# Rows of turns in DRAM once instead of twice, and stacked queries by two transfers instead of four

## The chip, the cores and the metric

The kernel runs on one core of one Trainium2 chip. The time is device microseconds (us) of a whole execution. The kernel before took 3939.81 us, the median of three runs between 3923.31 and 3940.42. Profiles come from one execution; a "line" (L951) is a line of the kernel's source.

## The reference

A single layer of a vision transformer runs on 16 images of 512 x 512, each cut into N = 1024 patches of 768 values and embedded to E = 256. The part that this change touches is attention with 8 heads of 32, whose keys go through a Fourier series before they meet the queries:

```
q, k, v = split(layernorm(h) @ w_qkv)            # 8 heads of 32
k = sum over f = 1..256 of kan_a[f]*sin(f*k) + kan_b[f]*cos(f*k)
h = h + softmax(q @ k.T / sqrt(32)) @ v @ w_out + b_out
h = h + shared_mlp(layernorm(h)) + two best of four experts(layernorm(h))
```

Everything is float32. Per image there are 256 x 1024 key values, each with 256 sines and 256 cosines.

## The kernel before

**The series.** The 256 frequencies are split into products of slow and fast waves. A key value is turned into a whole number of 2^-32 turns (the *turns*, `ui`), and a second one a quarter turn ahead (`uh`); the product of such an integer with a frequency wraps by itself. Eight key rows (`e`) make a group `g`; an image has 32 groups (`NG`) and the kernel 512. A group has two tiles `w` of 128 lanes x 1024 (j = 0, 1) of slow waves, four rows each, and one tile `f` of fast waves. Each goes through POOL (turn times the lane's frequency, L1006), ACT (sine, L1016), and then PE mixes the two w tiles (`mix`, L1036), DVE multiplies by f (L1050), and PE adds up (`add_up`, L1069). Four groups make a *round*; there are 128, and one step of attention (`att`: a pair of heads and half of the queries) runs two rounds behind its keys: eight score steps (L1134), eight exponentials (L1149), eight weighings of the values (L1167).

**Through DRAM.** A lane of a w tile needs one of four rows, with or without the quarter turn, so rows have to be spread over lanes. This goes through DRAM:

- `keys` (L564 to L607) computes turns of 128 rows x 512 columns and writes `uh` and `ui` to `ud[E, 2, 2, N]`: row, quarter or not (`f`), copy (`i`), column. Both copies come from one transfer that reads its source twice.
- `load_waves` (L942 to L956) fills a w tile by two loads, one for each half of the columns. The source is four rows x 2 x 2 copies = 16 rows of DRAM, each read by 8 lanes: a pattern of [16, 8, 512] with stride 0 in the middle; the destination is 128 partitions. There are 2048 such loads of 256 KB. A load waits until both halves of its rows are written and, with eight w tiles, until the mix of four groups before has freed its tile.
- `load_source` (L958 to L984) loads `src`, from which DVE spreads the fast waves' rows. It reads copy 0 in 512 loads of 64 KB, whose source pattern leads with the eight groups.
- `queries` (L619 to L641) writes queries, split into a high and a low part, to `qd[2, E, N]`. `stack_queries` (L1106 to L1122) fills `q4[128, 2, 512]` for one step of attention: for the high and the low part (j), each twice (x), 32 partitions. A score step multiplies it with stacked keys `k4`.
- `finish_keys` and `stack_keys` (L1082 to L1102) do the like for keys, by way of `kd`.

**What sets the order.** The order of PE's work is written out in a string (`ORDER`), one letter or digit for each step. The order on SP, POOL, ACT and DVE is made at build time by a planner (`others`, L408): it gives each step a cost and a time at which its dependencies are done, and takes the step that can start soonest. All of these transfers are issued by SP, in the planner's order; SP waits at each until what it depends on is done. `sent` and `transfer` (L312 to L320) are the planner's costs of transfers, and the numbers given to `put` those of issuing. They set the place of a step in its queue, and nothing on the chip.

Of the kernel before, what the change touches and what calls it, by code (L numbers as in the profile page):

```python
# [11 lines left out]
FP = mybir.dt.float32  # L12
# [6 lines left out]
P = 128  # L19
E = 256  # L20
NPAIR = 4
HD = 32
N = 1024
# [17 lines left out]
INT = mybir.dt.int32  # L41
# [10 lines left out]
PE, ACT, DVE, POOL, SP = "pe", "act", "dve", "pool", "sp"  # L52
# [38 lines left out]
def plain_path(ctx: ExitStack, tc: tile.TileContext, a: dict, out: bass.AP, verdict: bass.AP):  # L91
# [9 lines left out]
    nc = tc.nc  # L101
    xT = a["xT"]
    B = xT.shape[0]
    NG = N // P * 4

    def pool(name, bufs, space=None):
        kw = {} if space is None else {"space": space}
        return ctx.enter_context(tc.tile_pool(name=name, bufs=bufs, **kw))
# [4 lines left out]
    udp = pool("udp", 2, DRAM)  # L113
    qdp = pool("qdp", 2, DRAM)
# [17 lines left out]
    def load(shape, src, name):  # L132
        t = const.tile(shape, FP, tag=name, name=name)
        nc.scalar.dma_start(out=t, in_=src)
        return t
# [4 lines left out]
    def halves(src):  # L140
        return src.rearrange("(c p) e -> p c e", p=P)
# [4 lines left out]
    w_qkv = a["w_qkv"]  # L146

    wk = load([P, 2, E], halves(w_qkv[:, E : 2 * E]), "wk")
    wq = load([P, 2, E], halves(a["wq"]), "wq")
# [20 lines left out]
    for i in range(4):  # L170
        nc.scalar.dma_start(out=biases[ds((NE + 1) * i, NE), 0, :], in_=a["eb3"])
        nc.scalar.dma_start(
            out=biases[ds((NE + 1) * i + NE, 1), 0, :], in_=a["sb3"].unsqueeze(0)
# [78 lines left out]
    done = {}  # L252
# [8 lines left out]
    def put(engine, queue, cost, deps, key, action):  # L261

        queues[engine].setdefault(queue, []).append((cost, deps, key, action))
# [29 lines left out]
    def side_tile(name):  # L293

        i = chains[now["chain"]]["bank"] = banks(now["chain"])[0][1]
        return side.tile([P, 512], FP, tag=f"side{i}", name=name)
# [15 lines left out]
    def transfer(took, issue=0.0, ready=0.0):  # L312

        clock[SP] = max(clock[SP], ready) + issue
        now["dma"] = max(now["dma"], clock[SP]) + took
        return now["dma"] + LANDS

    def sent(took, issue):

        return transfer(took, issue, chains[now["chain"]]["ready"])  # L320
# [154 lines left out]
    images = [{} for _ in range(B)]  # L475
# [88 lines left out]
    def keys(b, rows, blks=(0, 1)):  # L564

        st = images[b]
        if b >= 2:
            yield "load", NG * (b - 1) - 1, 1
            yield "source", (NG * (b - 1)) // 8 - 1
        if "ud" not in st:  # L570
            st["ud"] = udp.tile([E, 2, 2, N], INT, tag="ud", name="ud")
        for blk in blks:
            yield "hnT", b, blk
            yield ANY
            ps = side_tile("k")
            for c in range(2):
                matmul(
                    out=ps,
                    lhsT=wk[:, c, ts(rows, P)],
                    rhs=hnT[:, c, ts(blk, 512)],  # L580
                    start=(c == 0),
                    stop=(c == 1),
                )
            held = chains[now["chain"]]["bank"]
            yield DVE, 1.4
            chains[now["chain"]]["bank"] = held
            u = rup.tile([P, 512], FP, tag="u", name="u")
            n = u.bitcast(INT)
            nc.vector.tensor_scalar(n, ps, INV_2PI, None, ALU.mult)
            nc.vector.scalar_tensor_tensor(ps, n, -TWO_PI_A, ps, ALU.mult, ALU.add)  # L590
            yield DVE, 1.4
            chains[now["chain"]]["bank"] = held
            for part in (TWO_PI_B, TWO_PI_C):
                nc.vector.scalar_tensor_tensor(ps, n, -part, ps, ALU.mult, ALU.add)
            yield DVE, 1.4
            ui = rup.tile([P, 512], INT, tag="r", name="ui")
            uh = n
            nc.vector.tensor_scalar(u, ps, INV_2PI_REST * 2.0**31, None, ALU.mult)
            nc.vector.scalar_tensor_tensor(ui, ps, INV_2PI * 2.0**31, u, ALU.mult, ALU.add)
            yield POOL, 1.02  # L600
            nc.gpsimd.tensor_tensor(uh, ui, quarter.to_broadcast([P, 512]), ALU.add)
            for i, x in enumerate((uh, ui)):
                nc.sync.dma_start(
                    out=st["ud"][ts(rows, P), i, :, ts(blk, 512)],
                    in_=x.unsqueeze(1).to_broadcast([P, 2, 512]),
                )
            done["rows", b, rows, blk] = sent(2.7, 1.2)  # L607

    def split(src, name):

# [8 lines left out]
    def queries(b, rows):  # L619
        st = images[b]  # L620
        for half in range(2):
            yield "hnT", b, half
        if b >= 2:
            yield "q", 2 * NPAIR * (b - 1) - 1
        if rows == 0:
            st["qd"] = qdp.tile([2, E, N], FP, tag="qd", name="qd")
        for blk in range(2):
            yield ANY
            ps = side_tile("q")
            for c in range(2):  # L630
                matmul(
                    out=ps,
                    lhsT=wq[:, c, ts(rows, P)],
                    rhs=hnT[:, c, ts(blk, 512)],
                    start=(c == 0),
                    stop=(c == 1),
                )
            yield DVE, 1.4
            for i, x in enumerate(split(ps, "q")):
                nc.sync.dma_start(out=st["qd"][i, ts(rows, P), ts(blk, 512)], in_=x)  # L640
            done["queries", b, rows] = sent(1.4, 1.0)  # L641

    def values(b):
# [294 lines left out]
    def rows_of(g):  # L938
        b, g = divmod(g, NG)
        return [("rows", b, g // (NG // 2), blk) for blk in range(2)]  # L940

    def load_waves(g, j):  # L942


        def action():
            w = w_tiles[g, j] = wp.tile([P, N], INT, tag="w", name="w")
            ud = images[g // NG]["ud"]
            src = ud[ds(8 * (g % NG) + 4 * j, 4)].rearrange("e f i n -> (e f i) n")
            for c in range(2):
                part = src[:, ts(c, 512)].unsqueeze(1).to_broadcast([16, 8, 512])  # L950
                nc.sync.dma_start(out=w[:, ts(c, 512)], in_=part)  # L951
            done["loaded", g, j] = transfer(1.9)

        old = g - NW // 2
        deps = rows_of(g) + ([("mix", old)] if old >= 0 else [])
        put(SP, "waves", 1.1, deps, ("load", g, j), action)  # L956

    def load_source(p):  # L958


        def part(j, blk):
            def action():
                if j == blk == 0:
                    sources[p] = srcp.tile([P, 2, 512], INT, tag="src", name="src")
                ud = images[p // NPAIR]["ud"]
                rows = ud[ts(p % NPAIR, 64), :, 0, :].rearrange(
                    "(g j r e) f n -> j r g e f n", j=2, r=2, e=2
                )
                for r in range(2):
                    nc.sync.dma_start(  # L970
                        out=sources[p][ds(64 * j + 32 * blk, 32), r, :],
                        in_=rows[j, r, :, :, :, ts(blk, 512)],
                    )
                landed = transfer(0.4)
                if j == blk == 1:
                    done["source", p] = clock[SP]
                    done["angles", p] = landed

            return action

        deps = rows_of(8 * p) + [("spread", 8 * p - 1) if p > 0 else ("load", 0, 1)]
        for j in range(2):
            for blk in range(2):
                put(SP, "source", 1.4, deps, ("part", p, j, blk), part(j, blk))  # L984
# [121 lines left out]
    def stack_queries(att):  # L1106
        p, qb = divmod(att, 2)
        b, i = divmod(p, NPAIR)

        def action():  # L1110
            q4 = bands_of_queries[att] = q4p.tile([P, 2, 512], FPR, tag="q4", name="q4")
            for j in range(2):
                src = images[b]["qd"][j, ts(i, 64), ts(qb, 512)]
                for x in range(2):
                    nc.sync.dma_start(
                        out=q4.bitcast(FP)[ds(64 * j + HD * x, HD), :, :],
                        in_=src.rearrange("(s d) n -> d s n", s=2),
                    )
            done["q4", att] = transfer(1.6)

        deps = [("queries", b, i // 2)] + ([("score", att - 2, NT - 1)] if att > 1 else [])
        put(SP, "queries", 2.0, deps, ("q", att), action)  # L1122


    scores = {}
# [110 lines left out]
    for j in range(XBUFS):  # L1236
        load_x(0, j)
    feed(1, first_norm(0, 0), keys(0, 0, [0]))
    feed(0, first_norm(0, 1), keys(0, 0, [1]))
    for b in range(B):  # L1240
# [29 lines left out]
    for rd in range(B * RI + 2):  # L1270
        groups = range(GS * rd, min(GS * rd + GS, total))
        att = rd - 2
# [706 lines left out]
def _places():  # L1979

    d = np.arange(HD)
    return d // 16 * 8 + d // 8 % 2 * 2 + d // 4 % 2 * 16 + d // 2 % 2 * 4 + d % 2
# [56 lines left out]
```

## Time and profile before

| What | Before |
|---|---|
| Median of three runs | 3939.81 us |
| The profiled execution: its own time, and its span from the first to the last instruction | 3924.07 us, 3922.5 us |
| Granted TensorE clock, mean | 0.994 |
| Data moved by transfers | 916.51 MB, 234 GB/s on average |
| HBM read, written | 758.64 MB, 150.99 MB |
| Issue of one w load on SP, of one q load, of one src load (median) | 544 ns, 419 ns, 652 ns |
| First and last issue of a w load, from the span's start | 57.2 us, 3791.8 us |
| PE: weighing of values, scores, mixes (busy) | 1269.7 us, 707.6 us, 540.1 us |
| POOL: turns of w and f (busy) | 2893.8 us |

PE is the tensor engine (PEld its weight loads), ACT the scalar, DVE the vector, POOL the GpSimd and SP the sync engine; SPq is SP's queue, where transfers are issued. `w<-ud` is a transfer into tile w from ud. A row of waits names who waited, for whom, the time in all, how often, and the longest. The chain that ended last goes back from the last instruction to what released it, step by step, and gives the share of the span that each engine or line has in it. The share of a DMA queue is the time that its packets took, out of the time of 16 DMA engines.

### The profile page before, as it was taken

How to read it: one execution, taken by the hardware profiler on the slowest of the kernel's cores; microseconds unless marked ns; L12 is line 12 of the kernel's file. 1: busy time of each engine (PE TensorE's matmuls, PEld its weight loads, DVE VectorE, ACT ScalarE, POOL GpSimd, SP SyncE). 2: the span in 40 equal slices, each digit the busy share in tenths (PEclk: the TensorE clock that was granted, in tenths of full speed). 3: DMA queues.
4: the chain of work that ended last, by engine and by line, in shares of the span. 5: the costliest groups of instructions: out<-in, count | busy, mean ns of one | idle time of the engine just before them, and what ended most of it. 6: DMA issues, size and time to landing. Idle time of an engine off the chain costs nothing.

```text
span 3922.5 us, 102737 instructions
## 1 busy us (share of the span) xinstructions
PE 3810.0 (97%) x40337; PEld 1948.9 (50%) x40337; DVE 2531.7 (65%) x4075; ACT 3263.0 (83%) x3939; POOL 3193.6 (81%) x2328
## 2 busy tenths in 40 slices
PE   7899999999999999999999999999999999999998
PEld 4334454554545555455454545545455454544444
DVE  4656757667675766757667675776767767576652
ACT  2788888888888888888888888888888888888983
POOL 3998878788788878879788788878879888888860
PEclk9999999999999999999999999999999999999999
DMA  7987968888787888979889788798878889788860
GB/s 228 281 261 217 278 192 245 259 226 258 220 257 225 237 264 224 259 216 256 235 233 265 212 257 247 224 265 224 262 218 255 247 229 265 216 245 235 221 170 18
DMA packets 587615, 916.51 MB, mean 234 GB/s; under 512 B 58828, under 2 KB 177524, under 8 KB 587124
## 3 DMA queue, kind: packets, MB, share of 16 engines
q1 hardware_dynamic: 580880, 906.98, 80.6%
q8 instruction: 321, 5.26, 0.6%
q10 hardware_dynamic: 6244, 2.88, 0.3%
q14 instruction: 170, 1.39, 0.1%
HBM read 758.64 MB, written 150.99 MB: 232 GB/s over the span
## 4 chain that ended last, share of the span: by engine, by line
PE 66%; DMA 13%; ACT 8%; POOL 5%; DVE 4%; issue 3%; SPq 2%; ACTq 0%; POOLq 0%; DVEq 0%
PE av L1167 17%; PE sT L1134 10%; PE kan L1036 8%; DMA w<-ud 7%; PE red L1069 4%; PE e1p L301 3%; PE tok L301 3%; ACT w L1016 3%; POOL w L1006 3%; PE e3p L301 2%; PE tok L304 2%; DMA k<-kd 2%; PE s1p L301 2%; PE e1p L304 2%; ACT f L1016 2%
## 5 line engine op out<-in xcount | busy, mean ns | idle before, releaser
L1006 POOL TENSOR_TENSOR w<-w,lane 128x1024 int32<-128x1024 int32 x1024 | 1923.6, 1895 | 406.9 <-DMA w<-ud 275.7
L1149 ACT ACTIVATE es<-sT 128x1024 f32<-128x1024 f32 x1024 | 1014.3, 1022 | 357.3 <-PE sT L1134 312.2
L1016 ACT ACTIVATE w<-w 128x1024 f32<-128x1024 int32 x1024 | 1013.4, 1046 | 67.5 <-POOL w L1006 64.3
L1006 POOL TENSOR_TENSOR f<-f,lane 128x1024 int32<-128x1024 int32 x512 | 970.2, 1895 | 102.0 <-DVE f L991 84.8
L1134 PE MATMUL sT<-q,k 128*128 128x512 f32 x2048 | 707.6, 454 | 42.9 <-DMA k<-kd 13.4
L1050 DVE TENSOR_TENSOR f<-kan,f 128x1024 f32<-128x1024 f32 x512 | 605.2, 1214 | 203.1 <-ACT f L1016 116.3
L991 DVE STREAM_SHUFFLE f<-src 128x1024 int32<-128x1024 int32 x512 | 681.3, 1370 | 0.4
L1167 PE MATMUL av<-es,v 128*32 128x256 f32 x8192 | 638.8, 383 | 3.5 <-DVE rc L1208 2.6
L1167 PE MATMUL av<-es,ones 128*32 128x256 f32 x8192 | 630.9, 379 | 0.0
L1036 PE MATMUL kan<-w,coef 64*32 64x512 f32 x8192 | 540.1, 598 | 18.8 <-ACT w L1016 12.6
L1016 ACT ACTIVATE f<-f 128x1024 f32<-128x1024 int32 x512 | 519.0, 1046 | 4.1 <-POOL f L1006 4.1
L1134 PEld LDWEIGHTS sT<-q,k 128*128 128x128 f32 x2048 | 351.2, 190 | 340.0 <-issue 146.0
L1167 PEld LDWEIGHTS av<-es,v 128*32 128x32 f32 x8192 | 235.5, 109 | 343.2 <-issue 236.9
L1167 PEld LDWEIGHTS av<-es,ones 128*32 128x32 f32 x8192 | 267.2, 110 | 176.4 <-issue 1.4
L1191 DVE RECIPROCAL rc<-av 128x256 f32<-128x256 f32 x128 | 224.8, 1756 | 169.5 <-PE av L1167 169.5
L1036 PEld LDWEIGHTS kan<-w,coef 64*32 64x32 f32 x8192 | 129.1, 105 | 313.9 <-issue 133.4
L1069 PE MATMUL red<-f,pack 128*32 128x512 f32 x2048 | 271.0, 602 | 0.0
L301 PE MATMUL tok<-wt,x 128*128 128x256 f32 x768 | 182.1, 389 | 22.1 <-DMA w1s<-in_sW 12.5
L1016 ACT ACT_TABLE_LOAD x128 | 164.2, 1283 | 17.7 <-DMA w<-ud 15.5
L304 PE MATMUL tok<-wt,x 128*32 128x256 f32 x3072 | 178.0, 380 | 0.6 <-DVE h L548 0.6
L301 PEld LDWEIGHTS tok<-wt,x 128*128 128x128 f32 x768 | 147.4, 194 | 57.9 <-DMA w1s<-in_sW 12.4
L513 ACT ACTIVATE hn<-h,less,rstd 128x256 f32<-128x256 f32 x256 | 140.7, 591 | 39.8 <-POOL less L505 39.0
(148 smaller groups left out, 4269.5 us busy)
## 6 DMA issues: line engine op xcount, KB each, us to landing
w<-ud SPq DMA_DIRECT2D x2048, 256.0 KB
q<-qd SPq DMA_DIRECT2D x512, 128.0 KB
k<-kd SPq DMA_DIRECT2D x128, 512.0 KB
x<-in_xT SPq DMA_DIRECT2D x128, 384.0 KB
ud<-u SPq DMA_DIRECT2D x64, 512.0 KB
ud<-ui SPq DMA_DIRECT2D x64, 512.0 KB
src<-ud SPq DMA_DIRECT2D x512, 64.0 KB
qd<-qhi SPq DMA_DIRECT2D x64, 256.0 KB
```

What stands on the lines that cost most here:

```text
L301: nc.tensor.matmul(out=out, lhsT=lhsT, rhs=rhs, start=start, stop=stop)
L304: nc.tensor.matmul(out=out[ts(i, 32)], lhsT=lhsT[:, ts(i, 32)], rhs=rhs, start=start, stop=stop)
L991: nc.vector.stream_shuffle(w, sources[g // 8].rearrange("p r n -> p (r n)"), [4 * (g % 8) + i // 8 for i in range(32)],)
L1006: nc.gpsimd.tensor_tensor(w, w, f.to_broadcast([P, N]), ALU.mult)
L1016: nc.scalar.activation(x, w, AF.Sin, scale=TURN * 2.0**-32)
L1036: nc.tensor.matmul(out=ps[ds(64 * j + 32 * blk, 32), ts(r, 512)], lhsT=coef[ts(r, 64)].rearrange("p e f j -> p (e f j)"), rhs=w[ts(r, 64), ...
L1050: nc.vector.tensor_mul(w, kan.pop(g), w)
L1069: nc.tensor.matmul(out=rows_of_pair[p][ts(2 * i + r, 32), :], lhsT=pack[:, ds(PACK0 - 16 * (k % 2) - 2 * (k // 2), 32)], rhs=prod[:, ts(r, ...
L1134: nc.tensor.matmul(out=ps[:, ts(s, 512)], lhsT=k4[:, 2 * s + kc // 4, ts(kc % 4, P)], rhs=q4[:, s, :], start=True, stop=True,)
L1149: nc.scalar.activation(es, scores.pop(kc), AF.Exp, scale=SCALE)
L1167: nc.tensor.matmul(out=acc[0][ts(i, HD), ts(half, 256)], lhsT=ones32 if half else v[:, kc, p % NPAIR, ts(i % 2, HD)], rhs=es[:, ds(512 * ( ...
L1191: nc.vector.reciprocal(rc[0], acc[0][:, 256:512])
```

## The change

Turns' rows are written to DRAM once: `ud` loses its dimension of copies, and the write of a half of the rows goes from 512 KB to 256 KB. A w load has now 8 rows of DRAM, each read by 16 lanes: the source pattern goes from [16, 8, 512] to [8, 16, 512]. The bytes that a load puts into the tile stay the same, and so does the order of the lanes.

Queries lie in DRAM by halves of the columns and with the two heads of a pair interleaved (a row is d, then s), for which the columns of `wq` are put in another order before launch. A head pair's high or low part is then 32 runs of 1024 values, and one load fills 64 partitions by reading them twice: the source pattern leads with a dimension of size 2 and stride 0. A step of attention takes two loads of 256 KB instead of four of 128 KB.

The planner's costs of the rows' writes and of stacked queries are smaller; `ORDER` is the same.

```diff
-            st["ud"] = udp.tile([E, 2, 2, N], INT, tag="ud", name="ud")
+            st["ud"] = udp.tile([E, 2, N], INT, tag="ud", name="ud")
...
             for i, x in enumerate((uh, ui)):
-                nc.sync.dma_start(
-                    out=st["ud"][ts(rows, P), i, :, ts(blk, 512)],
-                    in_=x.unsqueeze(1).to_broadcast([P, 2, 512]),
-                )
-            done["rows", b, rows, blk] = sent(2.7, 1.2)
+                nc.sync.dma_start(out=st["ud"][ts(rows, P), i, ts(blk, 512)], in_=x)
+            done["rows", b, rows, blk] = sent(1.4, 1.0)
...
-            st["qd"] = qdp.tile([2, E, N], FP, tag="qd", name="qd")
+            st["qd"] = qdp.tile([2, 2, E, 512], FP, tag="qd", name="qd")
...
-                nc.sync.dma_start(out=st["qd"][i, ts(rows, P), ts(blk, 512)], in_=x)
+                nc.sync.dma_start(out=st["qd"][i, blk, ts(rows, P)], in_=x)
...
-            src = ud[ds(8 * (g % NG) + 4 * j, 4)].rearrange("e f i n -> (e f i) n")
+            src = ud[ds(8 * (g % NG) + 4 * j, 4)].rearrange("e f n -> (e f) n")
             for c in range(2):
-                part = src[:, ts(c, 512)].unsqueeze(1).to_broadcast([16, 8, 512])
+                part = src[:, ts(c, 512)].unsqueeze(1).to_broadcast([8, 16, 512])
                 nc.sync.dma_start(out=w[:, ts(c, 512)], in_=part)
...
-                rows = ud[ts(p % NPAIR, 64), :, 0, :].rearrange(
+                rows = ud[ts(p % NPAIR, 64)].rearrange(
                     "(g j r e) f n -> j r g e f n", j=2, r=2, e=2
                 )
...
-                src = images[b]["qd"][j, ts(i, 64), ts(qb, 512)]
-                for x in range(2):
-                    nc.sync.dma_start(
-                        out=q4.bitcast(FP)[ds(64 * j + HD * x, HD), :, :],
-                        in_=src.rearrange("(s d) n -> d s n", s=2),
-                    )
+                src = images[b]["qd"][j, qb, ts(i, 64)].rearrange("(d s) n -> d (s n)", s=2)
+                nc.sync.dma_start(
+                    out=q4.bitcast(FP)[ts(j, 64)].rearrange("p s n -> p (s n)"),
+                    in_=src.unsqueeze(0).to_broadcast([2, HD, 1024]),
+                )
...
-        put(SP, "queries", 2.0, deps, ("q", att), action)
+        put(SP, "queries", 1.1, deps, ("q", att), action)
...
-    heads = np.arange(0, E, HD)[:, None]
-    arrays["wq"] = arrays["w_qkv"][:, (heads + _places()).ravel()]
+    heads = np.arange(0, E, HD).reshape(NPAIR, 1, 2)
+    arrays["wq"] = arrays["w_qkv"][:, (heads + _places()[:, None]).ravel()]
```

## The prediction

> **What bounds the kernel now.** I read the page from the top: busy shares, slices, DMA queues, the chain that ended last. Then the list of DMA issues, the waits, and SP's queue in order of time in the middle of the run.
>
> Busy shares and DMA queues of the kernel before (share of the span; packets, MB, share of 16 DMA engines):
>
> ```profile
> PE 3810.0 (97%) x40337; PEld 1948.9 (50%) x40337; DVE 2531.7 (65%) x4075; ACT 3263.0 (83%) x3939; POOL 3193.6 (81%) x2328
> ...
> q1 hardware_dynamic: 580880, 906.98, 80.6%
> ...
> PE 66%; DMA 13%; ACT 8%; POOL 5%; DVE 4%; issue 3%; SPq 2%; ACTq 0%; POOLq 0%; DVEq 0%
> ```
>
> PE sets the pace (97%), at 3922.5/128 = 30.6 us for each of 128 rounds, but the 16 DMA engines are used to 80.6% *if the work is spread evenly over all of them*. There is room for a fifth more transfer time, not for twice as much on any one engine. The longest waits on a transfer, the issues (KB each), and SP's queue for one round (start, us, count):
>
> ```profile
> POOL w L1006 <- DMA w<-ud: 275.7, 98, 9.8
> ...
> w<-ud SPq DMA_DIRECT2D x2048, 256.0 KB
> q<-qd SPq DMA_DIRECT2D x512, 128.0 KB
> k<-kd SPq DMA_DIRECT2D x128, 512.0 KB
> ...
> src<-ud SPq DMA_DIRECT2D x512, 64.0 KB
> ...
> 1960.09 13.28 SPq L951 DMA_DIRECT2D w<-ud  x16
> 1978.85 2.12 SPq L1115 DMA_DIRECT2D q<-qd  x4
> 1985.38 5.62 SPq L970 DMA_DIRECT2D src<-ud  x8
> 1991.10 6.65 SPq L951 DMA_DIRECT2D w<-ud  x10
> ```
>
> The reader should see that w loads are 537 of the 916 MB, sixteen in each round, and that POOL already waits for them 276 us in all. From the landings (semaphore increments) I worked out what the page does not print. Back to back, a w load of 256 KB lands every 0.88 us (1511 pairs), a k load of 512 KB every 2.69 us. From the packet records: 512 B takes 27 ns, 1 KB 46 ns, 2 KB 84 ns as the commonest value, mean 104 when at most eight packets are in flight and 113 at sixteen.
>
> **What decides: over how many engines a transfer is spread.** [...] Every one of the 2048 w loads (source [16, 8, 512]) shows 16 increments, and every one of the 512 src loads, whose source pattern leads with g of size 8, shows 9: one lump and eight singles. That an outermost 8 gives eight engines is thus seen here; that an outermost 2 gives two[...] no run here shows yet.
>
> **The change part by part.** Per DMA engine; "engine 0" is one that every transfer uses. A round is one group of four (8 w tiles, 16 w loads).
>
> *w loads (line 950).* The source goes from 16 rows x 8 lanes to 8 rows x 16 lanes: k goes from 16 to 8, and each used engine moves 16 packets of 2 KB per load instead of 8. Lower bound: 16 x 84 ns + 11 ns for the increment = 1.36 us. Upper bound: double the present rhythm, 2 x 0.88 = 1.76 us. With fewer engines competing I take the middle, 1.56 us. Per round 16 x 1.56 = 25.0 us (21.8 to 28.2), against 16 x 0.88 = 14.1 now.
>
> *q loads (lines 1111 to 1118).* Four loads per round of 32 partitions each (k = 16) become two whose source leads with the stride-0 "2": k = 2. Each of the two engines moves 32 packets of 4 KB. The nearest row gives 27, 46, 84 ns for 512 B, 1 KB, 2 KB, some 38 ns per further KB, so 160 ns unobstructed. Upper bound: k loads, which write only partitions 0 to 63 or 64 to 127, need 2.69 us / 16 packets = 168 ns per 2 KB, twice the free value. [...] so 320 ns if both keep step. I take 220 ns: 2 x 32 x 0.22 = 14.1 us per round (10.2 to 20.5), against 4 x 0.53 = 2.1 now. The two issues saved per round (2 x 0.42 us of SP) are worth nothing, because SP would be waiting for landings.
>
> *Rows written once (lines 603 to 607).* 128 writes of 512 KB become 256 KB: 33.5 MB less of 916.5. On an engine 8 packets less per write: 128 x 8 x 0.10 = 0.1 ms in all, already taken off in the next sum. Hidden before under PE; without that cover it is the only gain of the change.
>
> *Unchanged on engine 0, per round:* one k load 2.7; one x load 48 x 31 ns = 1.5; four src loads 4 x 4 x 0.10 = 1.6; one each of ud, qd, kd writes 3 x 8 x 0.10 = 2.4; out 0.4; increments 0.3. Sum 8.9 us (8 to 9.5).
>
> *Not on the path:* the reordered wq columns are made on the host; the qd write keeps its 128 rows outermost and its 2 KB packets, so k = 16; the src load keeps its outermost 8. The planner's smaller costs may move side work by a place in the SP, POOL, ACT and DVE queues; PE's order is written out and stays. PE's slack of the new round, 48 − 30.6 us, hides that; without that cover I would bound it at ±20 us.
>
> *The sum.* 25.0 + 14.1 + 8.9 = 48.0 us per round on engines 0 and 1, beyond the 30.6 that PE needs. So the bound moves from PE to these two DMA engines. 128 x 48.0 = 6144 us. Around it, as in the profiled execution: 57 us before the first w load is issued and 3922.5 − 3791.8 = 131 us after the last: 6332. SP waits for kd to land before each stack of keys (121 us in 60 waits now); the queue is empty then and takes some 2 us to fill again: 64 pairs x 2.3 = 150. Total 6.48 ms, rounded to 6450, on the profiled execution's own 3924.07 us; the median of the three runs, 3939.81, is 0.4% above it, which is nothing beside this.
>
> **Can the engines stay busy?** SP's transfers rotate through eight semaphores, and each issue waits for the one eight before; eight w loads are 12 us of work on engine 0, so SP may stand for that long without emptying it. Behind a standing SP are the loads of the next round, whose tiles come free as the mixes of this round are done; mixes lie together at a round's start, and scores and weighted values, over 20 us of PE work, follow while the queue drains. That fits within 48 us. Late next, where it does not: POOL for w, then the sines, the mixes, and so the freeing of tiles.
>
> **Rivals.**
> 1. *Not slower: the outermost dimension does not matter, and all transfers still use 16 engines.* Place: line 950; price: none; it decides if a w load still posts 16 increments and lands every 0.9 us. Then the saved bytes (3.7% of the traffic) count: 3.7% of the DMA part of the chain (13% of 3922 = 510 us) is 19 us, some more from 256 fewer issues on SP: about 3890. Against it: the 9 increments of the src loads.
> 2. *Only the w loads are confined* (the leading 2 of q is folded or handled otherwise). Engine 0 per round 25.0 + 2 + 8.9 = 36, still over 30.6: 128 x 36 + 338 = 4.95 ms (4.6 to 5.2). [...]
> 3. *The confined loads hide under PE.* Engine 0 then has 39,936 packets of 2 KB (32,768 w, 2048 src, 2048 k, 1024 each ud, qd, kd) and 8192 of 4 KB, equal to 56,320 of 2 KB, beside 0.28 ms of small ones. To fit in 3.74 ms each would have to take at most 61 ns; the commonest, free, value is 84. Excluded.
> 4. *Worse than the sum:* [...] (q 20.5), w at 1.76, and SP stalled by waits for scores or kd with the queue empty, 4 us a round: 128 x (28.2 + 20.5 + 9.5 + 4) + 190 = 8.15 ms. For it: SP's waits on PE, kan 228 us and sT 162 us now.
>
> **How the numbers follow.** Forecast 0.78 (own range 5.3 ms from the lower bounds, 128 x 40.0 + 190, to 7.8 from the upper, 128 x 58.2 + 340); rival 4: 0.08; rival 2: 0.08; rival 1: 0.06, of which two thirds faster; rival 3: 0. A difference from no change can be told beyond 0.5%. The predicted time is the forecast's, 6450. The range 5000 to 7800 takes in the forecast's own range and the upper part of rival 2, some 8 in 10. Faster 0.04, same 0.02, slower 0.94.
>
> **What would show it.** Right: nine increments per w load (a lump and eight) and three per q load; w landings about 1.6 us apart; q landings 5 to 10 us apart; the DMA share falling to about 40% with fewer GB/s (883 MB in 6.45 ms is 137)[...]; PE's share near 60%, POOL's near 50%; the largest waits POOL for w<-ud, and "DMA" leading the chain. Wrong: 16 increments on w (rival 1), or 3 on q missing (rival 2); a DMA share that stays near 80%; or w at the forecast's rhythm but long gaps with no transfer in flight, which would put the time with SP's order and rival 4.

## The result, and the profile after

The changed kernel takes 5529.57 us (median of 4 runs, 5525.02 to 5531.43), against 3931.56 us (4 runs, 3923.06 to 3940.42) for the kernel before: 1.4068 times as long, 95% interval 1.4042 to 1.4094. The profiled execution took 5529.45 us, its span is 5527.9 us.

First the page of the changed kernel: busy shares, DMA queues, HBM, and the chain that ended last.

```profile
PE 4138.2 (75%) x40337; PEld 2057.4 (37%) x40337; DVE 2498.1 (45%) x4075; ACT 3288.4 (59%) x3939; POOL 3199.9 (58%) x2328
...
q1 hardware_dynamic: 524048, 873.33, 47.9%
...
HBM read 758.64 MB, written 117.44 MB: 158 GB/s over the span
...
DMA 53%; PE 22%; POOL 7%; ACT 6%; issue 4%; DVE 4%; SPq 4%; POOLq 0%; ACTq 0%; DVEq 0%
DMA w<-ud 24%; DMA kd<-klo 11%; DMA k<-kd 8%; PE sT L1130 5%; DMA q<-qd 4%; PE av L1163 4%; POOL w L1003 4%; DMA ud<-ui 3%; SPq L948 2%; PE kan L1033 2%; DMA ud<-u 2%; PE red L1066 2%; ACT w L1013 2%; ACT es L1145 1%; PE tok L304 1%
```

The reader should see two numbers that seem to contradict each other. The DMA share fell from 80.6% to 47.9%, and transfers went from 13% of the chain to 53%. Fewer bytes are written (117 MB instead of 151) and more time is lost. A *share of 16 engines* is a mean: it can hide that a few of them are full while the rest stand.

The two issues that the change touches, from the same page (count, KB each):

```profile
w<-ud SPq DMA_DIRECT2D x2048, 256.0 KB
q<-qd SPq DMA_DIRECT2D x256, 256.0 KB
```

The two longest waits of the changed kernel for a transfer (us in all, times, longest):

```profile
POOL w L1003 <- DMA w<-ud: 1609.9, 300, 22.1
...
PE sT L1130 <- DMA k<-kd: 620.0, 59, 21.7
```

And SP's queue in order of time, a little over one round in the middle (start, us, count):

```profile
2736.28 16.29 SPq L948 DMA_DIRECT2D w<-ud  x16
2753.31 1.73 SPq L1111 DMA_DIRECT2D q<-qd  x2
2759.01 0.34 SPq L1085 DMA_DIRECT2D kd<-khi  x1
2759.73 0.34 SPq L1085 DMA_DIRECT2D kd<-klo  x1
2772.11 1.20 SPq L1095 DMA_DIRECT2D k<-kd  x2
2773.41 19.00 SPq L948 DMA_DIRECT2D w<-ud  x16
```

POOL's wait for w went from 276 to 1610 us. In SP's queue kd is issued at 2759 and the stack of keys only at 2772, for kd lands behind the two q loads. From the trace's records of increments and packets I worked out what no view prints (a *lump* is the one increment that comes about a microsecond after the issue, well before the others: medians after the change 1.04 us for a w load, the next at 7.63; 0.95 us for a q load, the next at 13.52):

- All 2048 w loads show 9 increments (before: 16), all 256 q loads 3 (before: 16): one lump and eight, one lump and two. All 512 src loads still show 9, and kd writes, like k loads, 16. For every increment but a lump there is a packet of 4 bytes on SP's queue: 55,824 before (8 for each src load, 16 for any other transfer; 11.3 ns on average) and 31,760 after (8 for each w and src load, 2 for each q load, 16 for the rest). I read one such packet as one engine, so w runs on eight engines, and q on two.
- The two q loads just shown land at 2765.79 and 2770.76, kd at 2771.41 and 2772.05, though kd was issued at 2759 and a kd write before the change took 3.2 to 3.7 us at the median. Its increments tell on which engines it stood: of the first kd write's sixteen, fourteen came between 2760.90 and 2762.70, and the last two at 2770.84 and 2771.41, after both q loads. Two engines were taken, and the transfer that uses all sixteen was done only when these two were.
- Packets of SP's queue in flight, from its first packet to its last: none for 188 us (before 415), exactly two for 949 us (before 59), eight or nine for 2583 us (before 122), fifteen or more for about 670 us (before over 2500).

The last row is the result in one line: for a sixth of the time two engines work for q, for nearly half of it eight work for w. That two or eight packets in flight are two or eight engines is read from the increments; a packet's record does not name its engine.

For comparing runs I split the time from SP's first issue to the last landing by transfer: each gets the time from the landing before it, or from its own issue if that is later, to its own landing; what is left had no transfer issued and unfinished. A load issued on an idle path brings its latency into its number.

| Run | w loads: us, each | q loads: us, each | k loads, us | others, us | nothing in flight, us | sum, us |
|---|---|---|---|---|---|---|
| before | 1945, 0.95 | 318, 0.62 | 443 | 1038 | 173 | 3917 |
| after | 2917, 1.42 | 1447, 5.65 | 390 | 671 | 98 | 5523 |
| queries' half undone | 3052, 1.49 | 208, 0.41 | 426 | 740 | 107 | 4533 |
| rows' half undone | 1827, 0.89 | 1611, 6.29 | 404 | 798 | 187 | 4827 |
| w on four engines | 5350, 2.61 per 256 KB | 1406, 5.49 | 376 | 667 | 100 | 7899 |

### The profile page after: what moved, and what is told of

The parts are those of the page before. It is cut to its first block, busy times and chain, and to the rows that moved or that the text cites. A ratio compares the mean times of both kernels' runs of the same rounds, so it can differ in the third digit from the quotient of the medians.

```text
span 5527.9 us, 102483 instructions
## 1 busy us (share of the span) xinstructions
PE 4138.2 (75%) x40337; PEld 2057.4 (37%) x40337; DVE 2498.1 (45%) x4075; ACT 3288.4 (59%) x3939; POOL 3199.9 (58%) x2328
## 3 DMA queue, kind: packets, MB, share of 16 engines
q1 hardware_dynamic: 524048, 873.33, 47.9%
## 4 chain that ended last, share of the span: by engine, by line
DMA 53%; PE 22%; POOL 7%; ACT 6%; issue 4%; DVE 4%; SPq 4%; POOLq 0%; ACTq 0%; DVEq 0%
DMA w<-ud 24%; DMA kd<-klo 11%; DMA k<-kd 8%; PE sT L1130 5%; DMA q<-qd 4%; PE av L1163 4%; POOL w L1003 4%; DMA ud<-ui 3%; SPq L948 2%; PE kan L1033 2%; DMA ud<-u 2%; PE red L1066 2%; ACT w L1013 2%; ACT es L1145 1%; PE tok L304 1%
## 5 line engine op out<-in xcount | busy, mean ns | idle before, releaser
L1130 PE MATMUL sT<-q,k 128*128 128x512 f32 x2048 | 794.8, 501 | 817.5 <-DMA k<-kd 620.0
L1013 ACT ACTIVATE w<-w 128x1024 f32<-128x1024 int32 x1024 | 1025.9, 1048 | 302.6 <-POOL w L1003 288.4
L1130 PEld LDWEIGHTS sT<-q,k 128*128 128x128 f32 x2048 | 399.4, 217 | 1163.4 <-issue 736.2
L1163 PE MATMUL av<-es,v 128*32 128x256 f32 x8192 | 652.8, 391 | 45.1 <-ACT es L1145 28.1
L1033 PE MATMUL kan<-w,coef 64*32 64x512 f32 x8192 | 581.7, 615 | 94.8 <-ACT w L1013 88.6
L1066 PE MATMUL red<-f,pack 128*32 128x512 f32 x2048 | 301.3, 662 | 0.0
L612 DVE CAST qhi<-q 128x512 fp32r<-128x512 f32 x64 | 44.0, 687 | 403.9 <-PE q L301 201.0
```

The source lines that it names most:

```text
L1013: nc.scalar.activation(x, w, AF.Sin, scale=TURN * 2.0**-32)
L1033: nc.tensor.matmul(out=ps[ds(64 * j + 32 * blk, 32), ts(r, 512)], lhsT=coef[ts(r, 64)].rearrange("p e f j -> p (e f j)"), rhs=w[ts(r, 64), ...
L1066: nc.tensor.matmul(out=rows_of_pair[p][ts(2 * i + r, 32), :], lhsT=pack[:, ds(PACK0 - 16 * (k % 2) - 2 * (k // 2), 32)], rhs=prod[:, ts(r, ...
L1130: nc.tensor.matmul(out=ps[:, ts(s, 512)], lhsT=k4[:, 2 * s + kc // 4, ts(kc % 4, P)], rhs=q4[:, s, :], start=True, stop=True,)
L1163: nc.tensor.matmul(out=acc[0][ts(i, HD), ts(half, 256)], lhsT=ones32 if half else v[:, kc, p % NPAIR, ts(i % 2, HD)], rhs=es[:, ds(512 * ( ...
```

## The experiments

Three theories stood first. Theory 1: the packets on the engine that every transfer uses set the time. Theory 2: SP's order does, since keys wait behind queries. Theory 3: many lanes reading one row of DRAM are slow, on however many engines.

**The rows' half undone** (from the changed kernel):

```diff
-    src = ud[ds(8 * (g % NG) + 4 * j, 4)].rearrange("e f n -> (e f) n")
+    src = ud[ds(8 * (g % NG) + 4 * j, 4)].rearrange("e f i n -> (e f i) n")
-    part = src[:, ts(c, 512)].unsqueeze(1).to_broadcast([8, 16, 512])
+    part = src[:, ts(c, 512)].unsqueeze(1).to_broadcast([16, 8, 512])
...
```

(and ud written twice again)

> The changed kernel with the rows' half undone: rows written twice, w loads of 16 rows x 8 lanes; queries as changed. Theory 1 (the packets on the engine that every transfer uses set the time): per round w 11 to 14 us, q 2 x 5.07 = 10.1, the rest 7.6 + 0.7 for the second copy: 29.5 to 32.5, so 128 x that + 188 = 3.96 to 4.35 ms, and up to 0.43 ms of standing on top: 4.2 to 4.7 ms. Theory 2 (the order of SP: keys wait behind the queries' 10 us, and that wait is the loss): nearly all of the loss stays, 5.1 to 5.5 ms. Theory 3 (16 lanes reading one row of DRAM are slow, whatever the engines): 3.9 to 4.1 ms.

Measured: 4833.65 us, 1.2315 times before (1.2294 to 1.2335). Above theory 1's range, below theory 2's, far above theory 3's. The table says where theory 1 fell short: w is back at 0.89 us, but a q load takes 6.29 us from the landing before it instead of 5.07. Its floor counted packets back to back, and what it allowed for standing on top was too small by 0.13 ms.

**The queries' half undone** (from the changed kernel; the layout of qd and the columns of wq go back too):

```diff
-    src = images[b]["qd"][j, qb, ts(i, 64)].rearrange("(d s) n -> d (s n)", s=2)
-    nc.sync.dma_start(
-        out=q4.bitcast(FP)[ts(j, 64)].rearrange("p s n -> p (s n)"),
-        in_=src.unsqueeze(0).to_broadcast([2, HD, 1024]),
-    )
+    src = images[b]["qd"][j, ts(i, 64), ts(qb, 512)]
+    for x in range(2):
+        nc.sync.dma_start(
+            out=q4.bitcast(FP)[ds(64 * j + HD * x, HD), :, :],
+            in_=src.rearrange("(s d) n -> d s n", s=2),
+        )
```

> The changed kernel with the queries' half undone: four q loads of 32 partitions; rows written once, w loads of 8 rows x 16 lanes. Theory 1: per round w 16 x 1.286 = 20.6 us, q 1.4 to 2.1, the rest 7.6: 29.6 to 30.3, just under PE's 30.6: 4.0 to 4.4 ms, DMA share about 65%. Theory 2: 3.9 to 4.0 ms, since nothing blocks the keys. Theory 3: most of the loss stays, above 4.8 ms.

Measured: 4546.89 us, 1.1594 times before (1.1574 to 1.1613). So the rows' part alone costs some 0.62 ms and, by the run before, the queries' part alone 0.91: 1.53 of the 1.60 that both cost. The sum nearly holds, which speaks against one shared cause such as keys behind queries, and for two pieces of work laid end to end on one path. It lies above theory 1's range again, by 0.15 ms, far above theory 2's and below theory 3's: w loads, 1.286 us apart at the median after the change, are 1.49 us each here. The DMA queue of this run:

```profile
q1 hardware_dynamic: 548112, 873.36, 59.7%
```

**Only the w loads confined**, the rest of the kernel before (rows are still written twice, copy 0 is read):

```diff
-    src = ud[ds(8 * (g % NG) + 4 * j, 4)].rearrange("e f i n -> (e f i) n")
+    src = ud[ds(8 * (g % NG) + 4 * j, 4), :, 0, :].rearrange("e f n -> (e f) n")
-    part = src[:, ts(c, 512)].unsqueeze(1).to_broadcast([16, 8, 512])
+    part = src[:, ts(c, 512)].unsqueeze(1).to_broadcast([8, 16, 512])
```

> The kernel before, rows written twice and queries by four loads, but w loads read copy 0 alone, 8 rows x 16 lanes. Nine increments per w load. Theory 1: as with the queries' half undone, plus 128 x 8 packets x 84 ns = 0.09 ms where that engine binds: 4.05 to 4.5 ms. If the writes are hidden, the two runs agree within 0.5%.

Measured: 4619.15 us, 1.1788 times before (1.1757 to 1.1818), nine increments per w load. What a load reads and its pattern changed in two lines, with the same bytes loaded and the planner's costs as before, and it costs 18%. That too is above theory 1's range, by 0.12 ms. It is 72 us above the run before, which differs in the second copy and the planner's cost of it: near the 0.09 ms of the copy's packets. Where the transfers bind, writing twice seems to have that price; the run on 16 engines, below, shows none where PE binds.

**w on four engines** (from the changed kernel): each load cut in two, the same bytes, the same 16 lanes per row.

```diff
-    part = src[:, ts(c, 512)].unsqueeze(1).to_broadcast([8, 16, 512])
-    nc.sync.dma_start(out=w[:, ts(c, 512)], in_=part)
+    for x in range(2):
+        part = src[ts(x, 4), ts(c, 512)].unsqueeze(1).to_broadcast([4, 16, 512])
+        nc.sync.dma_start(out=w[ts(x, 64), ts(c, 512)], in_=part)
```

> The changed kernel with each w load cut into two of four rows x 16 lanes (64 partitions each); the same bytes, the same 16 lanes per row. Theory 1[...]: five increments per load, 32 packets of 2 KB on the same four engines for what were 16 on eight; w 41.2 us per round, sum 58.9, 128 x 58.9 + 188 = 7.7 ms, up to 8.2. If the two halves fell on different engines, or lanes per row were the cause (theory 3): 5.4 to 5.8 ms.

Measured: 7904.59 us, 2.014 times before (2.0106 to 2.0173); five increments per load. The page of this run, DMA queue and chain:

```profile
q1 hardware_dynamic: 524048, 873.33, 31.8%
...
DMA 77%; PE 9%; SPq 5%; ACT 3%; POOL 2%; DVE 2%; issue 1%; POOLq 0%; ACTq 0%; DVEq 0%
```

Same bytes and a DMA share that falls once more, while the time grows by 2.4 ms. Four or five packets are in flight for 5195 us. The two halves did not run beside each other on different engines: the loads land 1.28 us apart (median) for 128 KB, as they did for 256 KB on eight. So they used the same four, and still with 16 lanes per row the time went up as the engines were halved: theory 3 falls. The packets say so too. One of 2 KB, most of which are w's, takes 84 ns at its commonest with 8 lanes per row (the kernel before) and with 16 (after, and here), and its mean goes down: 113, 98 and 93 ns. This run hits theory 1's number; its w loads take 1.31 us each on average, near the median.

**Keys ahead of queries** (from the changed kernel), which only moves steps in SP's queue:

```diff
     deps = [("queries", b, i // 2)] + ([("score", att - 2, NT - 1)] if att > 1 else [])
+    if qb == 1:
+        deps.append(("k4", p))
```

> The changed kernel with one more dependency in the planner: queries of the second half of a pair are stacked after the pair's keys, so that keys no longer stand behind the queries' loads. No transfer changes. Theory 1: the packets' sum is the floor, 128 x 38.3 + 188 = 5.10 ms; of the 0.43 ms of standing some goes, 5.15 to 5.5 ms, and SP's wait for kd falls from 585 us to under 350. Theory 2: well below the floor, under 5.0 ms.

Measured: 5581.05 us, 1.4209 times before (1.4187 to 1.4232), so 1% slower than the change itself, and above theory 1's range by 0.08 ms. SP's waits of the changed kernel, for kd and for the keys' high part (khi), which DVE makes and SP then writes to kd:

```profile
SPq L1095 <- DMA kd<-klo: 585.2, 64, 15.2
...
SPq L1085 <- DVE khi L612: 83.1, 36, 21.8
...
SPq L1095 <- DMA kd<-khi: 11.7, 1, 11.7
```

and of this run:

```profile
SPq L1085 <- DVE khi L612: 263.9, 40, 21.3
...
SPq L1095 <- DMA kd<-klo: 193.8, 64, 8.6
...
SPq L1095 <- DMA kd<-khi: 87.5, 20, 8.0
```

Two waits of the engines in this run:

```profile
POOL w L1003 <- DMA w<-ud: 1890.0, 285, 24.6
...
PE sT L1132 <- DMA k<-kd: 159.7, 25, 11.2
```

The wait for kd fell, for both writes together from 597 to 281 us, and PE's wait for k from 620 to 160 us. The time did not fall: the engines have the same packets to move, SP now stands at khi instead (264 us for 83), and POOL waits longer for w (1890 us for 1610). Theory 2, which had asked for under 5.0 ms here, falls, by this run and by the two halves.

**The change on 16 engines**: rows written once, queries in runs of 4 KB, but no transfer confined.

```diff
-    src = ud[ds(8 * (g % NG) + 4 * j, 4)].rearrange("e f n -> (e f) n")
+    src = ud[ds(8 * (g % NG), 8)].rearrange("e f n -> (e f) n")
-    part = src[:, ts(c, 512)].unsqueeze(1).to_broadcast([8, 16, 512])
+    part = src[:, ts(c, 512)].unsqueeze(1).to_broadcast([16, 8, 512])
...
-    nc.sync.dma_start(
-        out=q4.bitcast(FP)[ts(j, 64)].rearrange("p s n -> p (s n)"),
-        in_=src.unsqueeze(0).to_broadcast([2, HD, 1024]),
-    )
+    for x in range(2):
+        nc.sync.dma_start(
+            out=q4.bitcast(FP)[ds(64 * j + HD * x, HD)].rearrange("p s n -> p (s n)"),
+            in_=src,
+        )
```

(and the planner's cost of stacked queries goes back to 2.0)

> What the change would be if all its transfers used 16 engines: rows written once, w loads of 16 different rows x 8 lanes (16 increments), queries by 4 KB runs in four loads of 32 partitions. It leaves out the right choice of rows: a w tile gets eight key rows, each by 8 lanes, in place of four by 16; the rest is computed as before. All theories that put the loss on engines: 3.87 to 3.94 ms, same as before to 1.5% faster, DMA share 73 to 79%. If the loss came from writing rows once or from the queries' layout, it stays above 4.2 ms.

Measured: 3927.54 us, 0.9992 times before (0.9983 to 1.0001).

```profile
q1 hardware_dynamic: 548112, 873.42, 78.8%
```

With sixteen engines the change is worth nothing and costs nothing: 33.5 MB of writes fewer do not show where PE binds. So the 41% comes with the confinement to fewer engines; rows written once and the queries' layout are not what costs it. Lanes per row are back at 8 here too, but the run on four engines has ruled them out.

**Only the queries' layout**, on the kernel before, in four loads of 32 partitions as above:

```diff
-    st["qd"] = qdp.tile([2, E, N], FP, tag="qd", name="qd")
+    st["qd"] = qdp.tile([2, 2, E, 512], FP, tag="qd", name="qd")
...
```

> The kernel before with only the queries' layout of the change (heads interleaved, runs of 4 KB), still in four loads of 32 partitions on 16 engines. 8 packets of 2 KB per engine and load become 4 of 4 KB at the most: same to 0.3% faster, 3.91 to 3.94 ms. If the layout itself costs anything, slower by over 0.5%.

Measured: 3927.68 us, 0.9997 times before (0.9987 to 1.0006). Longer runs in DRAM are worth nothing here.

**Keys ahead of queries in the kernel before**, the same edit as above:

> The kernel before with the same dependency, queries of a pair's second half after its keys. PE binds and SP has slack: same, 3.91 to 3.95 ms; the wait of SP for kd stays near 120 us. If keys behind queries cost the kernel before too, 0.5 to 1% faster.

Measured: 3963.76 us, 1.0092 times before (1.0076 to 1.0109). Slower by 0.9%, outside what I had expected. SP's wait for kd hardly moved (122 us for both writes before, 151 here), while its wait for khi went from 80 to 304 us: the order spared SP nothing and made it stand elsewhere. That this is what costs the 0.9% is likely, but not shown.

**Ten w tiles.** The two halves cost more than their packets, so I asked whether the ring of eight w tiles explains the rest.

```diff
-NW = 8
+NW = 10
...
-    wq = load([P, 2, E], halves(a["wq"]), "wq")
+    wq = wk
...
```

> The kernel with the queries' half undone (w loads on eight engines, 4546.89 us), and ten w tiles instead of eight. To make room, the weights of queries, values, output and shared first layer are all taken from those of the keys: this leaves out the right weights, and every instruction stays but four small loads at the start. Theory A (a ring of eight tiles: a round's loads can only start when the mixes, which lie together, have freed the tiles, and 20.6 us of loads with some 15 us of latencies around them make the round): part of the 0.6 ms goes, 4.0 to 4.3 ms, POOL's wait for w<-ud falls from 803 us to under 500. Theory B (SP's standing at kd, or the engine's packets alone): 4.5 to 4.6 ms.

> The changed kernel with ten w tiles, room made in the same way (the right weights left out). The packets' sum on the busiest engines is the floor, 5.10 ms. Theory A: of the 0.43 ms above it more than half goes, 5.15 to 5.35 ms. Theory B: 5.45 to 5.55 ms.

> The kernel before with ten w tiles, the right weights left out in the same way. PE binds at 97%: Theory A: POOL's 276 us of waits for w<-ud fall by half, PE gains at most its 3% idle: 3.85 to 3.92 ms. Theory B: same.

> Control for the three runs with ten tiles: the kernel before with eight w tiles and the weights of queries, values, output and shared first layer taken from those of the keys (the right weights left out). No instruction on the way changes but four small loads at the start: 3.92 to 3.94 ms.

Measured, as ratios to before: 1.1628 (1.1602 to 1.1654) with the queries' half undone, against 1.1594 with eight; 1.4087 (1.4063 to 1.4110) for the change, against 1.4068; 0.9954 (0.9940 to 0.9968) for the kernel before; control 0.9996 (0.9987 to 1.0005). The waits of the change with ten tiles:

```profile
PE sT L1130 <- DMA k<-kd: 912.2, 63, 24.6
...
POOL w L1003 <- DMA w<-ud: 725.1, 199, 17.8
```

POOL's wait for w fell from 1610 to 725 us, PE's for k rose from 620 to 912, and the time stayed. Theory A falls: here the larger buffer moved the wait and took nothing from the time. Only where the transfers do not bind, in the kernel before, are ten tiles worth 0.5%, and the room for them was made by leaving out weights, so that is no version to use. Of the runs, none that keeps the right rows and weights beats the kernel before.

## Why the prediction was right, step by step

**Right: what decides.** Engines per transfer (k in the prediction) by the outermost dimension of the source: 9 and 3 increments, as forecast. The trace before had shown only the eight of the src loads; that the q loads get two was my estimate until the result. In the traces an outermost 8 goes with 9 increments (w and src), 2 with 3 (q), 4 with 5 (halved w). The prediction's sum rests on one engine that every transfer uses, its "engine 0". The run on four engines shows that the same ones are taken each time, and so do the sixteen increments of a kd write (the high part; us after its first, medians of 64 writes):

| Run | Increments of a kd write |
|---|---|
| before | all sixteen within 0.9 |
| rows' half undone (q on two) | fourteen within 0.4, two at 6.0 and 6.6 |
| queries' half undone (w on eight) | eight within 0.2, eight from 2.9 to 4.3 |
| after (w on eight, q on two) | eight within 0.2, six from 1.2 to 2.5, two at 9.9 and 10.4 |
| w on four (q on two) | twelve within 0.2, two at 2.3 and 2.7, two at 11.6 and 12.3 |

The late ones are as many as the engines that w and q use, and q's two lie among w's eight, and among w's four. Which of the sixteen they are, no record here tells; 0 and 1 in the prediction are names.

**Right: the bound moves from PE to the engines that every transfer uses,** and the direction. The four rivals fall: 1 by the increments, and by the run on 16 engines, which is what it described; 2 by the 3 increments of q and by the 0.91 ms that the queries' half costs alone; 3 by the result; 4 by its two parts: q loads take 5.65 us and not the 10.25 of its 20.5 a round, and between the first w load's issue and the last one's landing only 3 us pass with no transfer under way, where it put 0.5 ms. "Can the engines stay busy" was answered rightly in the main: SP stands 597 us at kd, yet between the first and the last w load there are only 75 us without a packet in flight. The traces agree that an issue waits for the transfer eight before it: SP's transfers take eight semaphores in turn (3736 of 3744 steps before, 3480 of 3488 after), and every issue comes after the landing of the one eight before it (3737 of 3737 before, 3481 of 3481 after, by 0.016 us or more).

**Mis-sized: the sum, 6.48 ms for 5.53.** A loss of 2.5 ms was forecast, and it is 1.6. The terms, against the table (us in all):

| Term of the sum | Predicted | Measured | Difference |
|---|---|---|---|
| w loads, 2048 | 1.56 each, 3195 | 1.42 each, 2917 | −278 |
| q loads, 256 | 7.04 each, 1802 | 5.65 each, 1447 | −355 |
| the rest on engine 0 | 8.9 x 128 = 1139 | 390 + 671 = 1061 | −78 |
| ends and standing | 188 + 150 = 338 | 98 and 5 before the first issue and after the last landing | −235 |

All four err to the same side, so none hid another, and the sum of the prediction's own lower bounds, 5.31 ms, is nearer than its middle values. The largest is the step that took 220 ns for a packet of 4 KB. The commonest is 159 ns, the mean 183. The line through the three shorter sizes, 160 ns, was right, and the doubling, taken over from k loads (168 ns for 2 KB, against 84), mostly did not come: 79% of the packets took at most 170 ns, 7% over 300. For w the same: the lower bound, 1.36 us, was nearer than the doubled rhythm, and the median of back-to-back pairs, 1.286 us, lies below it: 80 ns for each of 16 packets, less than the commonest duration of one, so packets on an engine overlap somewhat (up to 25 are in flight on 16 engines). The last row has two reasons. Of the 182 us before the first w load's issue and after the last one's landing, some 80 are transfers that the round's sum holds already, so that part was counted twice. And the 150 us for a queue that stands empty at kd hardly came: of the 98 us with no transfer under way, 3 lie between the first and the last w load; part of the time to fill the queue again is in the rows of w and k.

**Also off:** w landings 1.29 us apart at the median for "about 1.6", DMA share 47.9% for "about 40%", 160 GB/s for 137, PE 75% for "near 60%" and POOL 58% for "near 50%". The shares and the rate follow in the main from the shorter time, PE's also from its clock (below). The effect of the planner's smaller costs was bounded at ±20 us and not measured by itself; with 16 engines, and the smaller cost of the rows' writes in it, all comes to 0.9992. That of the stacked queries was never run alone.

**Open:** why w loads with the queries' half undone take 1.49 us each on average and 1.30 at the median. In the changed kernel, after kd had emptied the path at 2772 us, the first w loads land 1.53 us apart, later ones about 1.25. Why the first are slower, no run tested. It also stays open why theory 1's ranges fell short by 0.08 to 0.15 ms in four runs: what is shown is which engines bind, and not every microsecond between their packets' sum and the time.

## What to carry to other kernels

Look at the outermost dimension of a transfer's source pattern before anything else: in these runs 8, 4 and 2 meant that many engines (9, 5 and 3 increments), and the same ones each time, while 16, 32 and 128 meant all (16 increments). The destination's was 32 or more in all of these, so what a small one does was not shown. A copy that looks wasteful, like the second one of `ud`, or two loads that look mergeable, like those of q, may be there to make that dimension large enough. When the mean DMA share falls and waits on transfers grow, count increments or packets in flight; here a larger buffer and another order only moved such a wait from one consumer to the next. The increments of a transfer on all engines, read one by one, show at once how many of them were taken.

## What the hardware showed beyond that

- An engine moved more when fewer worked. On 16 engines back-to-back w loads come every 0.88 to 0.90 us, some 110 ns for each of 8 packets; on eight every 1.286 us (median), 80 ns for each of 16. Half of the engines cost 1.4 to 1.5 times the time, not twice; from eight to four it was twice (1.28 us per 128 KB).
- PE's granted clock and PE's share of busy time were lower together, at the same work: 0.994 at 97% (before), 0.943 at 88% (queries' half undone), 0.915 at 84% (rows' half undone), 0.876 at 75% (after), 0.775 at 60% (w on four engines). Score matmuls of 454 ns took 501 after the change. Which of the two follows from the other was not shown: no run held the clock apart. That PE's busy time of 4138 us after the change, for the work of 3810 before, is more likely a consequence of the loss than its cause is my estimate, from the chain that ended last: 53% of it are transfers and 22% PE.
